# A four-layer graph network on one core: the prologue's order and the written-out order of all jobs of a pair are replaced

## The chip, the cores and the metric

The kernel runs on one core of a Trainium2 chip. The metric is the device time of one execution in microseconds; lower is better. The core has engines that run side by side, each with its own list of instructions that it executes in order: TensorE (PE; PEld is its weight load), VectorE (DVE), ScalarE (ACT), GpSimd (POOL) and SyncE (SP, which issues DMAs). ScalarE issues DMAs too. The engines wait for each other through semaphores only.

## The reference, cut to what matters

Input `x` is 32 graphs of 512 nodes with 64 features, all on one graph matrix `adj` (512 x 512, mostly zeros, symmetric in its zeros but not in its values). Four layers follow one another, each with a layernorm and a relu ahead of it and a residual sum behind it:

```python
# layer 0, three steps, node 0 of v set to the intervention value before
effects = einsum('nm,bmd->bnd', adj, v)
v = relu(concat([v, effects]) @ W1.T + b1) @ W2.T + b2
# layer 1, two steps
z = relu(einsum('mn,bnf->bmf', adj, z) @ weights[i])
# layer 2: eight heads of 64 -> 128, then one of 1024 -> 64
h = x @ W
s = where((h @ h.T) * adj == 0, -1e16, (h @ h.T) * adj)
out = softmax(s) @ h + b            # leaky relu (0.01) behind both
# layer 3, with the diagonal of adj set to 1
e = adj * leaky_relu(e_src[:, None] + e_dst[None, :], 0.2)
out = softmax(e) @ h + bias
```

Everything is float32. Nearly all the work is layer 2: for each graph and head, a 512 x 512 matrix of scores, its softmax, and the weighted sum of values.

## The kernel before, in words

**Tiling.** The 32 graphs are processed as 16 pairs. A pair has a *front* (layers 0 and 1, and the layernorm of layer 2; a generator `front`, L333 to L390, whose 25 steps are called F0 to F24), then eight *units* `Heads` (two graphs times four groups; one unit holds 8 blocks of 64 rows x 512 columns, stored as [128, 8, 512]: two heads of 64 rows each), then the second layer of attention as one unit `Out`, and layer 3 as one unit `Last`. A unit goes through these jobs, each a method of `Unit`, where the letter of the unit's slot is put behind the job's name:

- s0 to s3, `scores` (L427, L430): TensorE makes two row blocks of scores each: four float32 matmuls of 64x64 by 512 a block pair's half (eight in a job) and four bfloat16 matmuls that add a very negative number where the graph is zero, from the tiles I2b (a 64 x 64 identity, twice) and NEGM.
- r0 to r7, `maxima` (L448): VectorE multiplies a block by the graph (A2, in which a zero has been made a one) and takes the row maximum. After every second one POOL negates the two maxima (L455).
- x0 to x3, `exponentials` (L459): ScalarE takes exp with that bias, two blocks a job, and sums rows.
- nA and nB, `normalise` (L469, L471): VectorE's reciprocal of the sums, then four multiplications on POOL.
- t0 to t3, `turn` (L477): VectorE transposes 32 x 32 blocks, two row blocks a job.

Two units together are a `Two`, a sum over nodes numbered by slot (0, 1 for the first graph, 3, 4 for the second): vA to vD, `weigh` (L487), 64 matmuls of 32x64 by 256 each into four PSUM buffers, with the values `vq` as weights; us (L542), four ScalarE copies out of PSUM; w0, y0, w1, y1 (L521, L532), the heads' weight matrices and leaky relu; o and c (L550 to L566), the output projection and its sum in `cat`; then f and h, which make features and node order for `Out`. The values of a graph are 16 small DMAs on SyncE that reorder a tile into quarters of 32 rows (`quarters`, L293, issue L299): ZQ1 does it for the second graph of a pair (the first graph's come with F24), h0 and h1 for `Out`, oN for `Last` (32 there, with four more at L676). `Ends` weighs (L756) an `Out` and a `Last` unit together, as vA2 to vD2, with eu and er behind it; jobs oA to oN are layer 3's layernorm, features and node order. k and Y (L804, L814) multiply the features by the gram matrix G of each head. ZZ1 turns the second graph's features.

**Buffers.** Four PSUM buffers take scores (`ps_s`), four take everything else (`ps_m`, tile name `mm`), in rotation: a job that asks for one waits until the reader of its last occupant is done. Units share three tiles `sm`. Each reordered value tile has one buffer.

**Order.** Nothing is scheduled by a planner at run time. The kernel is cut into ticks, ten to a pair. The table `PLACES` gives for each job a tick, relative to its unit's or pair's own, and a rank. The jobs of a tick are recorded in the order of their ranks, and every engine executes its instructions in the order of the record. The last pair's jobs, and what is left of the pair before it, come in an order of their own, the list `TAIL`, whose tokens have an owner ahead of the colon: a digit for a unit of heads of the last pair, T and U for its sums, p and e for `Out` and `Last` in it, E for `Ends`, and r, q, s for the units that are left behind it.

**Prologue.** The DMAs (L123 to L154): SyncE loads x, the graph A, the net parameters, Wh in two halves, A2, the small vectors, W_out and A3; ScalarE loads W1 and W2 (L132, L133), the biases (L136, L137), the intervention value (L139) and b2 spread over all partitions (L140). Then the first pair's front runs step by step, and `among` names what is put in front of which step: `weights_turned` (transposes of W1 and W2, three copies on ScalarE), `biases`, `weights_joined` (the products W2 W1, and the two bias products), `graph_turned` (sixteen transposes of A into AT, four copies on ScalarE), `masks` (II, I2b, NEGM), `factors` (zeros of A2 into ones), `grams` (G) and `vectors` (layer 3's). The second pair's first six steps run from step 6 on.

Of the kernel before, what the change touches and what calls it, by code (L numbers as in the profile page):

```python
# [9 lines left out]
BF16 = mybir.dt.bfloat16  # L10
AF = mybir.ActivationFunctionType
ALU = mybir.AluOpType
AX = mybir.AxisListType

P = 128
# [6 lines left out]
def gnn_stack_kernel(  # L22
# [107 lines left out]
    for j, r in enumerate(R):  # L130
        for k in range(2):
            nc.scalar.dma_start(out=W1n[r, k, r], in_=W1[:, k * D : (k + 1) * D])  # L132
        nc.scalar.dma_start(out=W2n[r, r], in_=W2)  # L133
    for k, b in enumerate((b1, b2, b_out, bias3)):
        for r in R:
            nc.scalar.dma_start(out=rows[H + k : H + k + 1, r], in_=b.rearrange("(o d) -> o d", o=1))  # L136
    nc.scalar.dma_start(out=rows[0:H, :], in_=bh)  # L137
    for j in range(2):
        nc.scalar.dma_start(out=ivt[:, j, :], in_=iv)  # L139
        nc.scalar.dma_start(out=b2bc[:, 0, j, :], in_=b2.partition_broadcast(P))  # L140
# [27 lines left out]
    I2b = const.tile([P, D], BF16, name="I2b")  # L168
# [13 lines left out]
    def graph_turned():  # L182
        for s in range(NT):
            pt = mm_ps()
            for t in range(NT):
                nc.tensor.transpose(pt[:, blk(t)], A[:, t, blk(s)], ident)
            nc.scalar.copy(AT[:, s, :], pt)
# [7 lines left out]
    def weights_joined():  # L195
        pt = mm_ps()
        for k in range(2):
            nc.tensor.matmul(pt[:, blk(k)], lhsT=W2n, rhs=W1T[:, k, 0, :], start=True, stop=True)
        nc.tensor.matmul(pt[:, 2 * P : 3 * P], lhsT=b2rep, rhs=W1T[:, 1, 0, :], start=True, stop=True)
        nc.tensor.matmul(pt[:, 3 * P : 3 * P + 1], lhsT=W1T[:, 0, 0, :], rhs=b2c, start=True, stop=True)  # L200
        for k in range(2):
            nc.vector.tensor_copy(W1T[:, k, 1, :], pt[:, blk(k)])
        nc.vector.tensor_copy(ubc[:, 0, :], pt[:, 2 * P : 3 * P])
        nc.vector.tensor_tensor(b1s, pt[:, 3 * P : 3 * P + 1], b1c, ALU.add)

    def masks():
# [3 lines left out]
        nc.vector.tensor_copy(I2b, II[:, 0, :])  # L210
# [21 lines left out]
    def grams():  # L232
# [5 lines left out]
        nc.vector.tensor_copy(WT.rearrange("p h d -> p (h d)"), pt)  # L238
# [4 lines left out]
        nc.vector.tensor_copy(G.rearrange("p h d -> p (h d)"), pt)  # L243
# [552 lines left out]
    def keys(ua, ub):  # L796
# [28 lines left out]
        1: [biases, weights_joined, graph_turned],  # L825
        7: [masks],
        8: [lambda: factors(0)],
        9: [lambda: factors(1)],
        10: [lambda: factors(2)],
        11: [lambda: factors(3)],  # L830
        14: [grams],
        15: [vectors],
    }
    for n, _ in enumerate(first):
# [7 lines left out]
        "begina": (0, 20), "s0a": (0, 21), "s1a": (0, 27), "s2a": (0, 97), "s3a": (0, 147), "r0a": (0, 81),  # L842
        "r1a": (0, 139), "r2a": (0, 148), "r3a": (0, 163), "r4a": (0, 214), "r5a": (0, 237),
        "r6a": (0, 242), "r7a": (0, 308), "x0a": (0, 253), "x1a": (0, 293), "x2a": (0, 298), "x3a": (1, 74),
        "t0a": (1, 118), "t1a": (1, 186), "t2a": (1, 285), "t3a": (1, 284), "nAa": (0, 310),
        "nBa": (1, 145), "beginb": (-1, 295), "s0b": (-1, 296), "s1b": (-1, 309), "s2b": (0, 195),
        "s3b": (0, 108), "r0b": (0, 52), "r1b": (0, 54), "r2b": (0, 57), "r3b": (0, 155), "r4b": (0, 234),
        "r5b": (0, 281), "r6b": (0, 226), "r7b": (0, 228), "x0b": (0, 88), "x1b": (0, 255), "x2b": (0, 314),
        "x3b": (0, 252), "t0b": (1, 84), "t1b": (1, 117), "t2b": (1, 102), "t3b": (1, 172), "nAb": (0, 286),
        "nBb": (1, 6), "beginc": (-1, 223), "s0c": (-1, 241), "s1c": (-1, 224), "s2c": (0, 166),  # L850
        "s3c": (0, 170), "r0c": (0, 83), "r1c": (0, 86), "r2c": (-1, 287), "r3c": (0, 37), "r4c": (0, 194),
        "r5c": (0, 248), "r6c": (0, 180), "r7c": (0, 185), "x0c": (0, 178), "x1c": (0, 174),
        "x2c": (0, 302), "x3c": (1, 33), "t0c": (0, 236), "t1c": (0, 299), "t2c": (1, 275), "t3c": (1, 268),
        "nAc": (0, 208), "nBc": (1, 49), "begind": (-1, 273), "s0d": (-1, 274), "s1d": (0, 28),
        "s2d": (0, 136), "s3d": (0, 71), "r0d": (0, 26), "r1d": (0, 46), "r2d": (0, 59), "r3d": (0, 78),
        "r4d": (0, 153), "r5d": (0, 182), "r6d": (0, 140), "r7d": (0, 203), "x0d": (0, 60), "x1d": (0, 163),
        "x2d": (0, 209), "x3d": (0, 238), "t0d": (0, 319), "t1d": (1, 0), "t2d": (1, 29), "t3d": (1, 38),
        "nAd": (0, 262), "nBd": (0, 294), "begine": (0, 41), "s0e": (0, 42), "s1e": (0, 62),
        "s2e": (0, 159), "s3e": (0, 55), "r0e": (0, 44), "r1e": (0, 132), "r2e": (0, 112), "r3e": (0, 152),
        "r4e": (0, 211), "r5e": (0, 216), "r6e": (0, 76), "r7e": (0, 161), "x0e": (0, 204), "x1e": (0, 183),  # L860
        "x2e": (1, 1), "x3e": (0, 258), "t0e": (1, 93), "t1e": (1, 162), "t2e": (1, 212), "t3e": (1, 263),
        "nAe": (0, 246), "nBe": (1, 129), "beginf": (-1, 103), "s0f": (-1, 312), "s1f": (-1, 104),
        "s2f": (0, 87), "s3f": (0, 151), "r0f": (0, 22), "r1f": (0, 77), "r2f": (-1, 239), "r3f": (-1, 261),
        "r4f": (0, 95), "r5f": (0, 179), "r6f": (0, 167), "r7f": (0, 259), "x0f": (0, 250), "x1f": (0, 173),
        "x2f": (0, 272), "x3f": (0, 290), "t0f": (0, 315), "t1f": (1, 43), "t2f": (1, 114), "t3f": (1, 122),
        "nAf": (0, 270), "nBf": (1, 9), "beging": (-1, 256), "s0g": (-1, 257), "s1g": (-1, 277),
        "s2g": (0, 68), "s3g": (0, 2), "r0g": (-1, 297), "r1g": (-1, 301), "r2g": (-1, 307), "r3g": (0, 23),
        "r4g": (0, 169), "r5g": (0, 229), "r6g": (0, 126), "r7g": (0, 142), "x0g": (0, 15), "x1g": (0, 47),
        "x2g": (0, 255), "x3g": (0, 249), "t0g": (0, 300), "t1g": (0, 311), "t2g": (1, 63), "t3g": (1, 64),
        "nAg": (0, 232), "nBg": (0, 260), "beginh": (0, 11), "s0h": (0, 12), "s1h": (0, 39), "s2h": (0, 99),  # L870
        "s3h": (0, 113), "r0h": (0, 75), "r1h": (0, 98), "r2h": (0, 105), "r3h": (0, 115), "r4h": (0, 124),
        "r5h": (0, 164), "r6h": (0, 133), "r7h": (0, 146), "x0h": (0, 100), "x1h": (0, 131),
        "x2h": (0, 215), "x3h": (0, 184), "t0h": (0, 265), "t1h": (1, 65), "t2h": (0, 288), "t3h": (0, 306),
        "nAh": (0, 192), "nBh": (0, 230), "begini": (0, 4), "s0i": (0, 5), "s1i": (0, 8), "s2i": (0, 67),
        "s3i": (0, 106), "r0i": (0, 13), "r1i": (0, 14), "r2i": (0, 16), "r3i": (0, 53), "r4i": (0, 111),
        "r5i": (0, 121), "r6i": (0, 190), "r7i": (0, 191), "x0i": (0, 80), "x1i": (0, 119), "x2i": (0, 235),
        "x3i": (1, 40), "t0i": (1, 89), "t1i": (1, 130), "t2i": (1, 243), "t3i": (1, 271), "nAi": (0, 267),
        "nBi": (1, 90), "beginj": (-1, 221), "s0j": (-1, 222), "s1j": (-1, 289), "s2j": (0, 144),
        "s3j": (0, 120), "r0j": (-1, 279), "r1j": (0, 17), "r2j": (0, 56), "r3j": (0, 61), "r4j": (0, 171),
        "r5j": (0, 254), "r6j": (0, 210), "r7j": (0, 225), "x0j": (0, 109), "x1j": (0, 220),  # L880
        "x2j": (0, 305), "x3j": (0, 280), "t0j": (0, 313), "t1j": (1, 66), "t2j": (1, 72), "t3j": (1, 176),
        "nAj": (0, 264), "nBj": (0, 318), "vA0": (1, 177), "vB0": (1, 198), "us0": (2, 25), "w00": (2, 70),
        "y00": (2, 82), "w10": (2, 127), "y10": (2, 150), "k0": (-1, 321), "Y0": (0, 10), "vA1": (1, 149),
        "vB1": (1, 156), "us1": (1, 282), "w01": (2, 32), "y01": (2, 45), "w11": (2, 134), "y11": (2, 143),
        "k1": (-1, 128), "Y1": (-1, 141), "vA2": (1, 135), "vB2": (1, 168), "vA3": (1, 137),
        "vB3": (1, 219), "us3": (2, 24), "w03": (2, 48), "y03": (2, 94), "w13": (2, 138), "y13": (2, 181),
        "k3": (-1, 187), "Y3": (-1, 189), "vA4": (1, 213), "vB4": (1, 233), "us4": (1, 304), "w04": (2, 34),
        "y04": (2, 85), "w14": (2, 116), "y14": (2, 125), "k4": (-1, 269), "Y4": (-1, 322), "o01": (2, 196),
        "c01": (2, 205), "o03": (2, 188), "c03": (3, 92), "f0": (4, 240), "h0": (5, 51), "o11": (2, 247),
        "c11": (3, 31), "o13": (2, 206), "c13": (3, 3), "f1": (3, 7), "h1": (3, 165), "eu": (2, 79),  # L890
# [159 lines left out]
```

## Time and profile before

| what | value |
|---|---|
| time, median of three runs | 2334.38 us (2334.08 to 2336.33) |
| profiled execution, its own time | 2338.17 us |
| its span, first to last instruction | 2336.3 us |
| mean granted TensorE clock | 0.976 |
| PE busy | 2186.7 us (94%), 32683 matmuls |
| DVE busy | 1857.4 us (80%) |
| ACT busy | 1493.1 us (64%) |
| POOL busy | 1299.6 us (56%) |

The profile is of one execution. A line of it gives a group of instructions or one stretch: start, duration, engine, source line, operation, the tile written and the tiles read (out<-in), their shapes, and how many; in square brackets stands how long the engine was idle before it and what ended that wait. Line numbers are those of the kernel before. A granted clock of 1.00 is TensorE's full speed. A window's row gives the busy time of every engine in that stretch of the span. Busy time of an engine that waits nowhere else is not the whole story: an engine can be idle without any other being the worse for it.

### The profile page before, as it was taken

Reading aid. Unit: us, or ns where it says so; the run is one execution under the profiler, and the core shown is the slowest. Engines: PE = TensorE matmul, PEld = TensorE weight load, DVE = VectorE, ACT = ScalarE, POOL = GpSimd, SP = SyncE. Lnnn points to the kernel's source line nnn. Section 1 sums busy time; section 2 is a strip of 40 time slices with the busy share of each in tenths; the row PEclk is TensorE's granted clock in tenths of the full one; section 3 lists DMA queues with packets and bytes.
Section 4 is the critical chain, followed back from the end, with each engine's and each line's share of the span. In section 5 each row is a group of like instructions: output and inputs, shape, how many; then the busy total and the mean of one; then the engine's idle time right before and its main releaser. Section 6 shows DMA issues by size and latency. Waiting matters only on the chain.

```text
span 2336.3 us, 78517 instructions
## 1 busy us (share of the span) xinstructions
PE 2186.7 (94%) x32683; PEld 1172.3 (50%) x32683; DVE 1857.4 (80%) x4100; ACT 1493.1 (64%) x3752; POOL 1299.6 (56%) x2175
## 2 busy tenths in 40 slices
PE   6889999999999999999999999999999999999863
PEld 3435555555555555555555555555555555555342
DVE  3558788879888888988888898888888898887653
ACT  1346557667676766767676676767666676766544
POOL 2345465656666565565656466565656556655342
PEclk9899999999999999999999999999999999999886
DMA  5001111202121120212112021211202111211112
GB/s 122 11 15 21 25 20 23 42 14 39 21 41 26 24 42 13 41 21 39 25 27 40 13 42 21 37 25 29 39 15 42 20 31 25 31 32 19 22 25 46
DMA packets 279047, 70.20 MB, mean 30 GB/s; under 512 B 275100, under 2 KB 276132, under 8 KB 278692
## 3 DMA queue, kind: packets, MB, share of 16 engines
q1 hardware_dynamic: 277888, 65.02, 16.8%
q8 instruction: 256, 4.19, 0.8%
q14 instruction: 99, 0.81, 0.1%
q10 hardware_dynamic: 804, 0.17, 0.0%
HBM read 10.49 MB, written 4.19 MB: 6 GB/s over the span
## 4 chain that ended last, share of the span: by engine, by line
PE 76%; ACT 9%; DVE 6%; POOL 2%; SPq 2%; issue 1%; DMA 1%; ACTq 0%; DVEq 0%; POOLq 0%
PE s L427 20%; PE mm L487 17%; PE mm L317 9%; ACT sm L459 6%; PE mm L550 5%; PE mm L756 5%; PE mm L521 5%; PE s L430 5%; DVE sm L477 4%; PE mm L329 3%; PE mm L804 3%; SPq L299 2%; PE mm L363 1%; DVE sm L448 1%; PE mm L593 1%
## 5 line engine op out<-in xcount | busy, mean ns | idle before, releaser
L459 ACT ACTIVATE sm<-sm,nmx 128x512 f32<-128x512 f32 x1280 | 911.0, 720 | 238.5 <-POOL nmx L455 238.2
L471 POOL TENSOR_SCALAR sm<-sm,rs 128x512 f32<-128x512 f32 x1280 | 869.8, 699 | 149.1 <-DVE rs L469 109.0
L448 DVE CUSTOM_DVE_ANT_0 sm<-s,A 128x512 f32<-128x512 f32 x1152 | 734.0, 679 | 146.3 <-PE s L430 119.8
L477 DVE STREAM_TRANSPOSE sm<-sm 128x1024 f32<-128x1024 f32 x640 | 769.4, 1224 | 39.5 <-POOL sm L471 38.4
L427 PE MATMUL s<-ZZ,Y 64*64 64x512 f32 x4096 | 572.1, 605 | 24.9 <-ACT Y L814 14.0
L487 PE MATMUL mm<-sm,vq 32*64 32x256 f32 (+1 forms) x17152 | 502.7, 380 | 26.0 <-DVE sm L477 18.3
L455 POOL TENSOR_SCALAR nmx<-mx 128x2 f32<-128x2 f32 x640 | 148.3, 235 | 600.6 <-DVE mx L448 544.7
L487 PEld LDWEIGHTS mm<-sm,vq 32*64 32x64 f32 x17152 | 401.8, 135 | 141.7 <-issue 55.9
L427 PEld LDWEIGHTS s<-ZZ,Y 64*64 64x64 f32 x4096 | 146.9, 132 | 250.2 <-issue 112.9
L430 PE MATMUL s<-NEGM,I2b 64*64 64x512 bf16 x2304 | 257.9, 378 | 0.0
L459 ACT ACTIVATION_READ_ACCUMULATOR sm<-sm,nmx 128x1 f32 x1280 | 251.2, 196 | 0.0
L542 ACT COPY us<-mm 128x256 f32<-128x256 f32 x256 | 76.2, 382 | 156.6 <-PE mm L487 156.4
L317 PE MATMUL mm<-AT,v 128*128 128x512 f32 x384 | 173.6, 595 | 0.0
L532 ACT ACTIVATE y<-mm,cols 128x512 f32<-128x512 f32 x256 | 159.2, 684 | 11.1 <-PE mm L521 11.0
L268 POOL TENSOR_TENSOR xc<-x,nmu 128x512 f32<-128x512 f32 x48 | 54.8, 1141 | 192.1 <-DVE nmu L266 192.1
L430 PEld LDWEIGHTS <-I2b 64*64 64x64 bf16 x2304 | 81.0, 107 | 159.8 <-issue 159.2
L521 PE MATMUL mm<-us,Wh 64*64 64x512 f32 x1024 | 133.9, 592 | 23.1 <-ACT us L542 23.1
L277 POOL TENSOR_TENSOR r<-ve,mhalf 128x8 f32<-128x8 f32 x64 | 110.8, 1731 | 44.9 <-DVE ve L275 41.1
L756 PE MATMUL mm<-sm,vq 32*64 32x256 f32 x3712 | 118.0, 380 | 10.2 <-DVE sm L477 8.8
L550 PE MATMUL mm<-y,Wo_sb 128*64 128x512 f32 x512 | 126.9, 605 | 0.0
L317 PE MATMUL mm<-AT,z 128*128 128x512 f32 x256 | 120.1, 613 | 2.1 <-DVE z L281 1.4
L317 PEld LDWEIGHTS mm<-AT,v 128*128 128x128 f32 x384 | 73.2, 191 | 93.3 <-issue 91.7
(134 smaller groups left out, 2002.0 us busy)
## 6 DMA issues: line engine op xcount, KB each, us to landing
vq<-z SPq DMA_DIRECT2D x512, 32.0 KB, 1.9
vq<-hn SPq DMA_DIRECT2D x512, 32.0 KB, 1.9
vq<-h3n SPq DMA_DIRECT2D x512, 32.0 KB, 1.9
A<-in_adj_dram SPq DMA_DIRECT2D x5, 1024.0 KB
xt<-in_x_dram SPq DMA_DIRECT2D x32, 128.0 KB, 2.3
out_dram<-xo SPq DMA_DIRECT2D x32, 128.0 KB, 2.9
src<-src SPq DMA_DIRECT2D x64, 1.0 KB, 1.9
Wh<-in_L_gnn_Wh_dram SPq DMA_DIRECT2D x2, 256.0 KB
```

Of the source, the lines that this page charges most:

```text
L317: nc.tensor.matmul(pe, lhsT=v[:, m].rearrange("p j d -> p (j d)"), rhs=AT[:, m, :], start=(first and m == 0), stop=(m == NT - 1),)
L427: nc.tensor.matmul(pss[half][R[ab], :], lhsT=lhsT, rhs=rhs, start=True, stop=False)
L430: nc.tensor.matmul(pss[half][R[ab], :], lhsT=I2b[R[half], :], rhs=NEGM[R[half], k, :], start=False, stop=True,)
L448: nc.vector.tensor_tensor_reduce(self.sm[:, s, :], src, graph, 1.0, -FMAX, ALU.mult, ALU.max, self.mx[:, s : s + 1])
L459: nc.scalar.activation(self.sm[:, s, :], self.sm[:, s, :], AF.Exp, bias=self.nmx[:, s : s + 1], accum_out=self.ssum[:, s : s + 1],)
L471: nc.gpsimd.tensor_scalar(self.sm[:, s, :], self.sm[:, s, :], self.rs[:, s : s + 1], 1.0, ALU.mult, ALU.mult)
L477: nc.vector.transpose(out=two, in_=two)
L487: nc.tensor.matmul(self.u[i][R[c], 0 : weights.shape[1] * 32], lhsT=values[32 * i : 32 * i + 32, jb, :], rhs=weights[32 * i : 32 * i + 32, ...
L521: nc.tensor.matmul(py[c][r, :], lhsT=Wh2[R[c], 2 * (self.q - 1 + c) + ab, r], rhs=self.us[R[c], 2 * ab : 2 * ab + 2].rearrange("p i (s e) ...
L532: nc.scalar.activation(y, py[c], AF.Prelu, bias=cols[:, h : h + 1], alpha=0.01)
L550: nc.tensor.matmul(pa[R[ab], :], lhsT=Wo_sb[:, h, :], rhs=self.y[h], start=(k == 0), stop=(k == 1),)
L756: nc.tensor.matmul(self.u[i][r, 0 : N // 2], lhsT=values[i // 2][q, jb, :], rhs=sm[q, :, 32 * jb : 32 * jb + 32], start=(jb == 0), stop=(j ...
```

## The change

Nothing that is computed changes, and no matmul is added or taken away.

- **Loads on ScalarE's queue.** W1's two halves come in one three-dimensional DMA for each half of the partitions (two in all in place of four). The two DMAs of the intervention value move ahead of those of the biases. Behind them ScalarE makes I2b with two copies of 64 rows from the identity; VectorE's cast of I2b in `masks` goes.
- **`graph_turned`** runs ahead of step 1 alone, and its four copies go to ScalarE and VectorE in turns. The products of weights follow at step 2, the biases at step 3, and the bias products, now a function of their own (`biases_joined`), at step 5. `masks` moves from step 7 to 9, the four `factors` from 8 to 11 to 16 to 19, `vectors` from 15 to 17.
- **`grams`** writes its two results with ScalarE, not VectorE.
- **PLACES and TAIL** have new ranks throughout. Most jobs keep their tick. In TensorE's list of a middle pair the differences are few: s0b stands between vB4 and vC4 (behind vD4 before), s2b ahead of w14 and k1, s2f ahead of w01, F18 ahead of s2g, h0 ahead of s0i, oT and oW earlier. On the other engines: ScalarE takes x1g ahead of F18 and x0g behind it (x0g, x1g, F18 before), x3a ahead of us4; VectorE takes the reciprocal of nBe ahead of t0e, c01 behind that of nBd, F13 ahead of r0e; SyncE issues ZQ1 in tick 1 of its pair, not in tick 5.

```diff
-    for j, r in enumerate(R):
-        for k in range(2):
-            nc.scalar.dma_start(out=W1n[r, k, r], in_=W1[:, k * D : (k + 1) * D])
+    for r in R:
+        nc.scalar.dma_start(out=W1n[r, :, r], in_=W1.rearrange("o (k d) -> o k d", k=2))
         nc.scalar.dma_start(out=W2n[r, r], in_=W2)
+    for j in range(2):
+        nc.scalar.dma_start(out=ivt[:, j, :], in_=iv)
+
+    I2b = const.tile([P, D], BF16, name="I2b")
+    for r in R:
+        nc.scalar.copy(I2b[r], ident[r, r])
...
-        nc.scalar.dma_start(out=ivt[:, j, :], in_=iv)
         nc.scalar.dma_start(out=b2bc[:, 0, j, :], in_=b2.partition_broadcast(P))
...
-            nc.scalar.copy(AT[:, s, :], pt)
+            (nc.scalar.copy, nc.vector.tensor_copy)[s % 2](AT[:, s, :], pt)
...
-        nc.tensor.matmul(pt[:, 2 * P : 3 * P], lhsT=b2rep, rhs=W1T[:, 1, 0, :], start=True, stop=True)
-        nc.tensor.matmul(pt[:, 3 * P : 3 * P + 1], lhsT=W1T[:, 0, 0, :], rhs=b2c, start=True, stop=True)
-        for k in range(2):
             nc.vector.tensor_copy(W1T[:, k, 1, :], pt[:, blk(k)])
-        nc.vector.tensor_copy(ubc[:, 0, :], pt[:, 2 * P : 3 * P])
-        nc.vector.tensor_tensor(b1s, pt[:, 3 * P : 3 * P + 1], b1c, ALU.add)
+
+    def biases_joined():
+        pt = mm_ps()
+        nc.tensor.matmul(pt[:, 0:P], lhsT=b2rep, rhs=W1T[:, 1, 0, :], start=True, stop=True)
+        nc.tensor.matmul(pt[:, P : P + 1], lhsT=W1T[:, 0, 0, :], rhs=b2c, start=True, stop=True)
+        nc.vector.tensor_copy(ubc[:, 0, :], pt[:, 0:P])
+        nc.vector.tensor_tensor(b1s, pt[:, P : P + 1], b1c, ALU.add)
...
-        nc.vector.tensor_copy(I2b, II[:, 0, :])
...
-        nc.vector.tensor_copy(WT.rearrange("p h d -> p (h d)"), pt)
+        nc.scalar.copy(WT.rearrange("p h d -> p (h d)"), pt)
...
-        nc.vector.tensor_copy(G.rearrange("p h d -> p (h d)"), pt)
+        nc.scalar.copy(G.rearrange("p h d -> p (h d)"), pt)
...
     among = {
         0: [weights_turned],
-        1: [biases, weights_joined, graph_turned],
-        7: [masks],
-        8: [lambda: factors(0)],
-        9: [lambda: factors(1)],
-        10: [lambda: factors(2)],
-        11: [lambda: factors(3)],
+        1: [graph_turned],
+        2: [weights_joined],
+        3: [biases],
+        5: [biases_joined],
+        9: [masks],
         14: [grams],
-        15: [vectors],
+        16: [lambda: factors(0)],
+        17: [lambda: factors(1), vectors],
+        18: [lambda: factors(2)],
+        19: [lambda: factors(3)],
     }
...
     PLACES = {
...
```

The ranks that the text speaks of, as (tick, rank), before and after: s0b (-1, 296) and (-1, 251); vB4 (1, 233) and (1, 212); vC4 (1, 251) and (1, 269); x0g (0, 15) and (0, 150); x1g (0, 47) and (0, 22); F18 (6, 107) and (6, 103); s2g (0, 68) and (0, 107); s2f (0, 87) and (0, 28); w01 (2, 32) and (2, 29); F13 (4, 73) and (4, 83); r0e (0, 44) and (0, 92); h0 (5, 51) and (4, 310); nBe (1, 129) and (1, 112); t0e (1, 93) and (1, 127); ZQ1 (5, 36) and (1, 91). In TAIL, VectorE's maxima `r:r0f` and `r:r1f` move behind the transposes `p:t2f`, `p:t3f` and `e:t0e`, and unit e's maxima ahead of `p:r0f`:

```diff
-        p:t0f r:x0f p:x2f U:h0 p:nBf r:r4f r:r5f r:x2f r:r7f p:t1f e:t0e p:t3f p:t2f r:x3f r:nBf E:vA2 r:nAf
+        r:r6f r:s0f r:r7f p:nBf r:x2f U:h0 r:r3f r:x3f p:t0f p:t2f p:t3f r:x1f r:r0f r:r1f E:vA2 E:vB2 r:nBf
```

## The prediction

> **What bounds the kernel now.** I read the page's busy table, then the kernel cut into windows, then the waits and the timeline inside those windows where an engine other than TensorE decides.
>
> ```profile
> PE 2186.7 (94%) x32683; PEld 1172.3 (50%) x32683; DVE 1857.4 (80%) x4100; ACT 1493.1 (64%) x3752; POOL 1299.6 (56%) x2175
> ```
>
> TensorE is the bound: 94% of the span. The change removes no matmul, so it can only win TensorE's idle time, or time at a halved clock. The windows say where that is (columns: window, its length, busy time of PE, PEld, DVE, ACT, POOL, granted clock, DMA share, GB/s):
>
> ```profile
> 0.00:74.00 74.00, 42.17 (x185) 25.06 (x185) 23.45 (x46) 10.22 (x18) 20.73 (x29) 0.88 0.44 97
> 74.00:210.00 136.00, 123.83 (x1467) 60.81 (x1470) 91.55 (x207) 71.03 (x179) 67.22 (x125) 0.95 0.11 19
> 618.00:754.00 136.00, 133.49 (x2054) 71.70 (x2046) 115.58 (x255) 93.34 (x236) 81.64 (x136) 1.00 0.18 29
> 2114.00:2250.00 136.00, 112.36 (x1638) 55.25 (x1638) 96.67 (x218) 83.44 (x214) 59.69 (x114) 0.90 0.14 22
> ```
>
> A middle pair of graphs (one period is 135.4 us, thirteen such) keeps TensorE busy for 133.5 of 136 at full clock: about 2.5 us a pair to win, and 115.6 of VectorE close behind. The prologue (42 of 74) and the last pair (112 of 136, clock 0.90) are loose. In the middle pair the waits view gives TensorE's two largest named waits:
>
> ```profile
> PE mm L521 <- ACT us L542: 1.7, 1, 1.7
> PE s L427 <- ACT Y L814: 0.7, 1, 0.7
> ```
>
> In the last pair one DMA wait stands out. SyncE's timeline, then TensorE's:
>
> ```profile
> 2150.47 23.21 SPq L299 DMA_DIRECT2D vq<-h3n  x32
> 2173.78 10.24 SPq L299 DMA_DIRECT2D vq<-z  x16
> ```
> ```profile
> 2179.88 0.65 PE L487 MATMUL mm<-sm,vq 32*64 32x256 f32 x4
> 2180.98 0.61 PE L487 MATMUL mm<-sm,vq 32*64 32x256 f32 x2 [0.46 <-DMA vq<-z]
> 2183.53 6.64 PE L487 MATMUL mm<-sm,vq 32*64 32x256 f32 x122 [1.93 <-DMA vq<-z]
> ```
> ```profile
> 990.60 3.71 PE L487 MATMUL mm<-sm,vq 32*64 32x256 f32 x128
> ```
>
> The sixteen transfers of the second graph's values (job ZQ1) queue on SyncE behind 32 of job oN, are issued only at 2173.78 to 2184.0, and the first half of the weighing vA3/vB3 waits for them. It takes 2179.88 to 2190.09 = 10.2 us. The last line is the same 128 matmuls in a middle pair: 3.6 us to the next instruction. Besides the waits, the clock was 0.50 in 2183.5:2187 and 0.57 in 2187:2190 by the windows.
>
> **The change part by part.**
>
> *ZQ1 from tick 5 of its pair to tick 1.* Sixteen SyncE issues of 0.64 us (10.24/16) now stand ahead of h1 and oN. Their buffer is free after the previous pair's vD4, which ends at 2107.9, so they would be issued by about 2119, and h1, in tick 2, can be issued up to 10 us later; what it loads is weighed in tick 6 (vA2), four ticks of 13.5 us on. oN, in tick 3, finds SyncE free by then. Gain in the last pair: 10.2 - 3.6 = 6.6 us. VectorE does not give it back: after it VectorE waits 6.77 us (2220.68) and 3.11 us (2228.16) for TensorE. Middle pairs: nothing, as 990.60 has no wait on a DMA. Bounds: -6.6, and -2.4 if only the waits (0.46 + 1.93) go and the clock is half anyway. I take -6.4, nearest to the row of the middle pair.
>
> The clock's part leans on the rows: after waits of 2.02 us (ahead of 2176.82) and 1.93 us the clock was 0.50. The Trainium skill ("TensorE: Matmul & The Clock Gate", Part 1) says that the clock halves after an idle window of some 3.4 us, and no single wait here is that long; by that page the slow clock would not be owed to these waits, this step would be worth 2.4 us and the sum -2.3 in place of -6.3. I keep the row.
>
> *The order at the end (TAIL).* Maxima r0f and r1f of the last unit go behind the transposes p:t2f and p:t3f for which E:vA2 waits (8.8 us for VectorE, at 2247.63): two of 0.61 us = -1.2. Against it, six maxima of unit e now go ahead: up to 6 x 0.61 = 3.7 later for the rest, half of it in VectorE's idle 6.77 us. Bounds -3 and +2; I take -1.2. The chain after E:vA2 (88 us to the end) is the same in both.
>
> *Prologue: ScalarE's DMAs and the turned graph.* Two weight DMAs fewer (about 0.3 us each by the issues at L137 to L140); the table load moves off W1T's path:
>
> ```profile
> 12.53 1.28 ACT L179 ACT_TABLE_LOAD   x1 [12.53 <-DMA ivt<-_intervention_value_dram]
> 13.82 0.43 ACT L179 COPY W1T<-mm 128x128 f32<-128x128 f32 x2
> 15.87 3.31 PE L186 MATMUL mm<-ident,A 128*128 128x128 f32 x16
> 19.69 0.59 ACT L311 COPY zT<-mm 128x512 f32<-128x512 f32 x1
> ```
>
> The graph's transposes need only A (9.25) and could go 5 us earlier; the four copies of 0.58 us are shared by two engines. What counts is the zT copy at 19.69, from which the first pair's chain runs. A new wait stands against it: the DMAs for b2bc share, in the program as built, a semaphore lane with Wh's second half and wait on ScalarE for its landing, with W1T, W2T and AT queued behind them. Wh's halves are issued at 12.46 and 13.11 now and landed at 20.4 and 21.5, some 8 us later; issued near 10, as nothing but the DMAs ahead of it on SyncE holds it, the second may land between 13.5 and 18.4. That puts zT 2.8 us earlier to 1.2 later; I take 0.8 earlier. Then biases_joined (matmuls 0.63 + 0.43) stands in the chain: +0.9. Factors move to steps 16 to 19: VectorE's 1.23 + 2.34 at 31.52 and 33.53 no longer hold the second chain: -1.1. Vectors at step 17: one TensorE wait for w3T, +0.65. Grams on ScalarE: -0.1. Removed cast (1.04 at L210): beside other work, 0. Sum -0.45; bounds -2.5 and +1.6; say -0.5. First pairs afterwards: 0 to +1, as their jobs are pulled between the two fronts; +0.3.
>
> *The middle pair's order.* TensorE's list is nearly the same; what differs:
> - s0b (eight matmuls and four masks) goes between vB4 and vC4, where the 256 matmuls were one run of 7.16 us. Split runs with scores between cost 990.60 to 999.11 = 8.51, less 1.23 for the scores = 7.28, and a boundary each: +0.1 to +0.3; I take +0.27, as vC4 starts after a change of tile.
> - ScalarE takes x1g before F18 and x0g after it. x1g waits for POOL's negation at 961.73 (behind nBf, 2.69 us), while x0g ran at 960.84. ScalarE then loses 1.1 us there and has 0.7 of slack before 965.11; x2g ends 0 to 0.5 later, and VectorE's reciprocal for it already waits:
>
> ```profile
> 968.07 0.18 DVE L469 RECIPROCAL rs<-ssum 128x4 f32<-128x4 f32 x1 [1.99 <-ACT sm L459]
> 968.17 4.74 DVE L477 STREAM_TRANSPOSE sm<-sm 128x1024 f32<-128x1024 f32 x4
> ```
>
>  Behind it stand t0g to t3g, r0h to r3h, s3h, F20 and vA3. I take +0.44.
> - Gains: s2f before w01 covers the 1.72 us wait, yet vA2 is held by VectorE's t3f, 0; F18 before s2g frees vA2's PSUM slot (0.6 lost there): half, -0.3; F13 before r0e frees vA1's (0.3): -0.3; h0 before s0i covers Y's 0.7, but vA3 waits for F20 and t1h (7.4 us of VectorE work) anyway: 0.
>
> Sum +0.1 a pair, +1.5 for thirteen. Bounds: -0.6 (both covered waits count too) to +0.71 (no gain comes).
>
> Total: -6.4 - 1.2 - 0.5 + 0.3 + 1.5 = -6.3. The profiled execution took 2338.2 (span 2336.3 + 1.9), 0.16% above the median of 2334.4; the terms are differences, so they go on the median: 2328.1.
>
> **The rivals.**
>
> *A, the loop eats the end.* The gains in the middle pair do not come: +0.71 x 13 = +9.2, and 2334.4 - 7.8 + 9.2 = 2335.8: no change. For it: in ticks 4 to 7 VectorE's chain (t3d, t3f, t3g, r3h) decides and TensorE's small waits fall there, so PSUM slots free earlier may help nobody. Against: 0.6 and 0.3 are waits on slots, not on VectorE.
>
> *B, slower: the reciprocal in front of the transposes.* In tick 5 VectorE now meets nBe's reciprocal ahead of t0e, in the stretch where it is the bound; if it waits for ScalarE there as at 968.07, it loses up to 1.99 us a pair with t0e, t3f and vA2 behind it. It decides from (4.7 + 7.8)/13 = 0.96 us; between the two, 1.5 x 13 = 19.5 gives 2346. Against it: ScalarE is 64% busy, and x2e may be done by then.
>
> *C, the values are hidden anyway.* vA3 needs t1h too, which ends near 2179.8. If the clock stays half for VectorE-bound reasons, only 2.4 is won: 2332.1, no change. For it: the clock is 0.90 over the whole window, so half clock exists without this wait.
>
> **How the numbers follow.** A measurement of this kernel tells 0.2% (4.7 us) from nothing. Forecast 0.45 (faster). A 0.22, of which 0.05 lies over +0.2%. B 0.23. C 0.10. Faster 0.45, same 0.27, slower 0.28. The forecast's own range is 2319 to 2331 (end -9, prologue -2.5 and -0.3 a pair below; +0.3 a pair above). The range reaches down to the end's -9.6 with prologue -2.5 and -0.6 a pair (-20: 2314.5), of which I keep 2315, and up into the lower half of B, 2345; outside lie about 0.06 and 0.12.
>
> **What would show it.** ZQ1: in the last pair, vA3 and vB3 in 3.6 us without a wait on a DMA, and the window at 0.9 clock or more; a half clock there with no wait is C. Loop: the period between two pairs' vA4 against 135.4; at 135.5 my sum is right, at 136.1 A, at 136.4 or more B, with an idle time ahead of L469 in tick 5. x1g: x2g's end against the start of its pair, +0.5. Prologue: zT's copy at about 18.9; W1T's first copy after a wait longer than now is the lane's doing. The forecast is wrong at once if the period moves by more than 0.4 us either way, since thirteen of them outweigh all else.

## The result and the profile after

The changed kernel takes 2343.99 us (median of six, 2340.26 to 2346.80) against 2334.43: ratio 1.0042, 95% interval 1.0031 to 1.0053. It is slower by some 10 us. The forecast was 2328, faster; the time lies inside the range given, 2315 to 2345, but only by what that range allowed for the slower rival B; the forecast's own range was 2319 to 2331.

The same four windows of the profile after (window, length, busy time of PE, PEld, DVE, ACT, POOL, granted clock, DMA share, GB/s):

```profile
0.00:74.00 74.00, 43.42 (x193) 26.18 (x197) 23.09 (x45) 11.17 (x21) 19.72 (x29) 0.86 0.44 98
74.00:210.00 136.00, 125.22 (x1533) 61.63 (x1534) 94.91 (x213) 73.19 (x185) 67.33 (x126) 0.95 0.11 18
618.00:754.00 136.00, 133.91 (x2019) 71.18 (x2003) 115.37 (x255) 93.51 (x235) 80.58 (x135) 1.00 0.18 29
2114.00:2250.00 136.00, 119.59 (x1790) 57.71 (x1790) 101.95 (x227) 85.00 (x217) 64.42 (x120) 0.92 0.13 21
```

The last pair's window is denser (119.6 of 136 busy, not 112.4; it begins 10.6 us earlier within that pair than before), the middle pair's looks the same. The busy share hides the loss; the distance from one pair's vA0 to the next shows it. TensorE's starts of vA0 in the timelines, and the stretches of the last pair, for the kernel before and for two profiled executions of the changed one (us):

| stretch | before | after, first | after, second |
|---|---|---|---|
| first vA0 begins | 107.8 | 105.7 | 108.0 |
| two first periods | 263.3 | 263.4 | 264.8 |
| a middle period, median | 135.29 | 136.31 | 136.30 |
| twelve middle periods | 1624.3 | 1636.1 | 1636.4 |
| last period | 129.5 | 130.4 | 130.7 |
| last pair, vA0 to vA3 | 54.9 | 55.8 | 54.2 |
| vA3 to vA4 | 25.2 | 18.5 | 18.5 |
| vA4 to vA2 of E | 42.5 | 39.7 | 39.6 |
| from there to the last issue on SyncE | 85.9 | 86.2 | 88.0 |

The last pair's vA3 to E's vA2 is 9.5 us shorter, a little more than forecast, and the period is 1.0 us worse, thirteen times. The profiled execution of the kernel before (2338.2) is 2 to 4 us above its medians, so differences of two profiled executions (+2.1 and +6.6) understate the loss; the medians are the measure.

ZQ1 did what was forecast. In the last pair SyncE has no z transfers behind oN's h3n transfers, and the first half of the weighing is one run of 3.71 us without a wait. TensorE's timeline after:

```profile
2191.07 0.38 PE L434 MATMUL s<-NEGM,I2b 64*64 64x512 bf16 x2
2191.38 3.71 PE L491 MATMUL mm<-sm,vq 32*64 32x256 f32 x128
2195.02 1.09 PE L431 MATMUL s<-ZZ,Y 64*64 64x512 f32 x8
```

In the middle pair both of TensorE's named waits are gone, and one of another kind stands there (waits view of after, PE's rows):

```profile
PE s L431 <- DVE mx L452: 1.6, 2, 1.3
PE mm L808 <- ACT ZZ L407: 0.2, 1, 0.2
```

Less is waited for by name (1.8 us against 2.4), and yet the period is longer. The page's chain of work that ended last shows where to look; before, then after:

```profile
PE 76%; ACT 9%; DVE 6%; POOL 2%; SPq 2%; issue 1%; DMA 1%; ACTq 0%; DVEq 0%; POOLq 0%
```
```profile
PE 53%; DVE 17%; ACT 13%; POOL 9%; issue 3%; SPq 3%; DMA 1%; DVEq 0%; ACTq 0%; POOLq 0%
```

The path has moved off TensorE for a fifth of the span: VectorE, ScalarE and POOL have a good part of it, although in the middle pair's window none of them has more to do than before (ScalarE 93.5 us, not 93.3). These shares do not say what it costs: with five orders put back, below, they are PE 65%, DVE 19%, POOL 7% and ACT 4%, and the period is within 0.15 us of the old one.

Laid side by side from vA4 on, two periods part like this: s0b to s1b +0.25; k3 to o03, behind vA1, a further 0.7; then VectorE's t0g is 0.90 later (84.52 us after vA4, not 83.62), F20 0.66 and t1h 0.66 later, and vA3, which waits for t1h, begins at 106.7, not 106.1; o11 adds 0.26. At the next vA4 the sum is 0.92 (1.02 by the medians).

The place behind vA1, ScalarE and TensorE, before and after:

```profile
812.18 1.09 PE L521 MATMUL mm<-us,Wh 64*64 64x512 f32 x8 [1.67 <-ACT us L542]
813.97 2.53 ACT L532 ACTIVATE y<-mm,cols 128x512 f32<-128x512 f32 x4
816.09 1.04 PE L804 MATMUL mm<-ZZ,G 64*64 64x256 f32 x16
817.07 1.94 PE L550 MATMUL mm<-y,Wo_sb 128*64 128x512 f32 x8
```
```profile
811.45 1.35 PE L431 MATMUL s<-HH 64*64 64x512 f32 x6 [1.28 <-DVE mx L452]
815.60 2.42 ACT L536 ACTIVATE y<-mm,cols 128x512 f32<-128x512 f32 x4
816.33 1.67 PE L808 MATMUL mm<-ZZ,G 64*64 64x256 f32 x16
817.93 1.94 PE L554 MATMUL mm<-y,Wo_sb 128*64 128x512 f32 x8
```

ScalarE takes x1f ahead of y01 after the change, so y01 and y11 begin at 815.60, not 813.97. TensorE's k3 (L808) takes 1.67 in place of 1.04 us, as it needs PSUM buffers that y01 empties, and o03 (L554), which multiplies the y, begins 0.86 later (0.99 counted from vA4, which stands at 749.23 before and 749.10 after).

### The profile page after: what moved, and what is told of

Its sections match the earlier page's. It is cut to its first block, busy times and chain, and to the rows that moved or that the text cites. A ratio compares the mean times of both kernels' runs of the same rounds, so it can differ in the third digit from the quotient of the medians.

```text
span 2338.5 us, 78505 instructions
## 1 busy us (share of the span) xinstructions
PE 2204.8 (94%) x32683; PEld 1174.0 (50%) x32683; DVE 1854.2 (79%) x4099; ACT 1503.7 (64%) x3754; POOL 1298.6 (56%) x2175
## 4 chain that ended last, share of the span: by engine, by line
PE 53%; DVE 17%; ACT 13%; POOL 9%; issue 3%; SPq 3%; DMA 1%; DVEq 0%; ACTq 0%; POOLq 0%
PE s L431 14%; PE mm L491 12%; ACT sm L463 9%; PE mm L321 8%; DVE sm L481 7%; DVE sm L452 6%; POOL sm L475 5%; PE mm L554 4%; PE s L434 3%; PE mm L525 3%; PE mm L808 3%; SPq L303 2%; PE mm L333 2%; ACT y L536 1%; PE mm L367 1%
## 5 line engine op out<-in xcount | busy, mean ns | idle before, releaser
L431 PE MATMUL s<-ZZ,Y 64*64 64x512 f32 x4096 | 577.4, 607 | 18.5 <-DVE mx L452 12.9
L491 PE MATMUL mm<-sm,vq 32*64 32x256 f32 (+1 forms) x17152 | 494.9, 378 | 25.4 <-issue 11.0
L491 PEld LDWEIGHTS mm<-sm,vq 32*64 32x64 f32 x17152 | 391.9, 134 | 145.3 <-issue 76.8
L431 PEld LDWEIGHTS s<-ZZ,Y 64*64 64x64 f32 x4096 | 141.9, 132 | 259.5 <-issue 96.8
L434 PE MATMUL s<-NEGM,I2b 64*64 64x512 bf16 x2304 | 268.7, 378 | 0.0
L525 PE MATMUL mm<-us,Wh 64*64 64x512 f32 x1024 | 139.8, 589 | 1.5 <-ACT us L546 1.5
L272 POOL TENSOR_TENSOR xc<-x,nmu 128x512 f32<-128x512 f32 x48 | 55.1, 1148 | 153.6 <-DVE nmu L270 153.6
L554 PE MATMUL mm<-y,Wo_sb 128*64 128x512 f32 x512 | 126.4, 607 | 3.3 <-ACT y L536 3.3
L473 DVE RECIPROCAL rs<-ssum 128x4 f32<-128x4 f32 x320 | 53.9, 168 | 90.0 <-ACT sm L463 89.8
L321 PEld LDWEIGHTS mm<-AT,v 128*128 128x128 f32 x384 | 73.3, 191 | 93.3 <-issue 92.3
```

The lines of the kernel that those rows point to most:

```text
L321: nc.tensor.matmul(pe, lhsT=v[:, m].rearrange("p j d -> p (j d)"), rhs=AT[:, m, :], start=(first and m == 0), stop=(m == NT - 1),)
L431: nc.tensor.matmul(pss[half][R[ab], :], lhsT=lhsT, rhs=rhs, start=True, stop=False)
L434: nc.tensor.matmul(pss[half][R[ab], :], lhsT=I2b[R[half], :], rhs=NEGM[R[half], k, :], start=False, stop=True,)
L491: nc.tensor.matmul(self.u[i][R[c], 0 : weights.shape[1] * 32], lhsT=values[32 * i : 32 * i + 32, jb, :], rhs=weights[32 * i : 32 * i + 32, ...
L525: nc.tensor.matmul(py[c][r, :], lhsT=Wh2[R[c], 2 * (self.q - 1 + c) + ab, r], rhs=self.us[R[c], 2 * ab : 2 * ab + 2].rearrange("p i (s e) ...
L554: nc.tensor.matmul(pa[R[ab], :], lhsT=Wo_sb[:, h, :], rhs=self.y[h], start=(k == 0), stop=(k == 1),)
```

## The experiments

**The changed kernel again, and two orders put back.**

```diff
-"x1f": (0, 31)     "s2f": (0, 28)
+"x1f": (0, 225.5)                       # e1 and e3
+                   "s2f": (0, 29.5)     # e2 and e3
```

> The changed kernel once more, for a second profile of it: its first profiled execution (2340.3 us) is the fastest of its six times (2340.3 to 2346.8). Theory P (the loss sits in the period of a middle pair, 136.3 against 135.3 us): the period is 136.3 again or a little more, and a slower time comes from longer periods (5 us over 13 pairs = 0.4 each). Theory V (the loss of the slower times sits at the ends, in prologue and last pair, where the granted clock is below 0.95): all periods 136.3 as before and the ends longer by up to 6 us.

> The changed kernel, with ScalarE's x1f put back behind y11 (rank 225.5 for 31). Theory X (x1f of 1.5 us ahead of y01 keeps two PSUM buffers that k3 waits for: k3 begins 0.24 and o03 0.86 us later than in the kernel before): the period falls from 136.3 by 0.8 to 0.9, to 135.4 or 135.5, and the time by some 11 us to 2333. Theory S (s2f ahead of w01 is the loss, since it waits 1.28 us for VectorE with w01 behind it): the period stays at 136.2 or more, and the time within 2 us of the changed kernel's.

> The changed kernel, with TensorE's s2f put back behind w01 (rank 29.5 for 28). Theory X: the period moves by at most 0.3, as k3 still waits for y01; time within 4 us of the changed kernel's. Theory S: the period falls by 0.8 or more, to 135.5 or less, and the time by 10 us or more.

> The changed kernel with both put back. Theory X: as with x1f alone, 135.4, or up to 0.3 less; time 2330 to 2333. Theory S: as with s2f alone. If neither is the loss, the period stays at 136.3.

| kernel | period | time | ratio to before |
|---|---|---|---|
| after, again | 136.30 | 2346.49 | 1.0043 (1.0028 to 1.0058) |
| x1f back | 136.05 | 2342.11 | 1.0024 (1.0014 to 1.0034) |
| s2f back | 136.96 | 2359.38 | 1.0096 (1.0081 to 1.0111) |
| both back | 136.92 | 2355.76 | 1.0088 (1.0072 to 1.0103) |

The second profile has the same period; what differs between executions lies at the ends (the first vA0 at 105.7 or 108.0, the last stretch 86.2 or 88.0). So P holds for the loss, and V, by these two profiles, for the scatter. Theory S falls with the wrong sign: s2f ahead of w01 is a gain of 0.65 us a period in this order (0.87 with x1f back as well), though its row shows a wait of 1.28 us that was not there before. Theory X has the right sign and a third of the size: 0.25, not 0.8 to 0.9; its bound on s2f, 0.3, does not hold either. With x1f back, o03 begins at 67.9 us after vA4, as before the change (67.8); 0.9 us are won there, and by vA3 0.6 of them are lost again. That a gain on TensorE vanishes before vA3 is the observation on which the next theory rests: that from there to vA3 VectorE sets the time.

**One order each, and five together.**

```diff
-"s0b": (-1, 251)  "x0j": (0, 138) "x1j": (0, 109)  "t0e": (1, 127)    "x0g": (0, 150)
+"s0b": (-1, 277.5)                                                    # e4, e9
+                  "x0j": (0, 109) "x1j": (0, 138)                     # e7, e9
+                                                   "t0e": (1, 111.5)  # e8, e9
+                                                                      "x0g": (0, 21.5)  # e9
+"x1f": (0, 225.5)                                                     # e9
```

> The changed kernel, with s0b put back behind vD4. Theory D (a period is one stretch that TensorE bounds, from vA3 to s0f, and one that VectorE bounds, from there to vA3; what is lost in either is paid in full, and TensorE's waits inside VectorE's stretch cost nothing): s0b's 0.25 us stands in TensorE's stretch, so the period falls from 136.30 to 136.05. Theory E (the period is TensorE's list with its waits added up): the same 0.25 less, so that this run alone does not tell them apart; it sets the price of the split.

> The changed kernel, with ScalarE's x0j and x1j exchanged, so that x0j stands ahead of y13 as before. x1j waits 0.91 us for POOL's negation there and y13, then o11 on TensorE, are 0.26 late. Theory D: that lies in TensorE's stretch, period 136.04. If the wait is taken over by another (k0, F6): 136.3.

> The changed kernel, with VectorE's t0e put back ahead of nBe's reciprocal, which waits 0.36 us for ScalarE at 65.2 of the period. Theory D: it lies in VectorE's stretch, and 0.14 to 0.36 of it come off the period: 135.9 to 136.2, though no wait of TensorE names it. Theory E: no change, 136.30, as no wait of TensorE goes.

> The changed kernel with five orders of the middle pair put back: s0b behind vD4, x1f behind y11, x0j ahead of x1j, t0e ahead of nBe, x0g ahead of x1g. The rest of PLACES, TAIL, ZQ1 and the prologue stay. Theory D: 136.30 less 0.25 (s0b), 0.25 (x1f, as measured), 0.26 (x0j), 0.14 to 0.36 (t0e) and 0 to 0.17 (x0g) gives 135.0 to 135.4, as before the change; then the changed ends are left, -6 to -8 us: ratio to the kernel before 0.9966 to 0.9980. Theory E: TensorE keeps the gains at vA1 and vA2 (0.55 and 0.24), which makes 134.6 to 134.9 and a ratio of 0.993 to 0.995.

The periods are 136.01 (s0b back), 136.11 (x0j first), 136.35 (t0e first) and 135.44 (all five). Each of the three single ones has one execution; the five measured 2332.81, ratio 0.9986 (0.9977 to 0.9996).

So s0b between vB4 and vC4 costs 0.30, x1j ahead of x0j 0.20, x1f ahead of y01 0.25: 0.75 of the 1.0. The last two are in the timeline of after: x1f above, and here x1j, ScalarE's wait for POOL, with y13 behind it, for which TensorE's o11 waits:

```profile
869.19 0.72 ACT L463 ACTIVATE sm<-sm,nmx 128x512 f32<-128x512 f32 x1 [0.91 <-POOL nmx L459]
870.62 1.24 ACT L536 ACTIVATE y<-mm,cols 128x512 f32<-128x512 f32 x2
871.67 1.51 PE L554 MATMUL mm<-y,Wo_sb 128*64 128x512 f32 x6
```

t0e, ahead of the reciprocal or behind it, is worth nothing in the changed kernel: with t0e first VectorE's wait of 0.36 us ahead of nBe goes, one of 0.30 comes behind r5f, its wait for TensorE's s0g ahead of r0g grows from 0.19 to 0.26, and r0g begins at 72.03 us after vA4, not 72.01. TensorE's late s0g (x1f, y, o03) set that time, not the reciprocal. The other 0.1 is left to x0g and the interplay of the five, by difference. In the kernel with five back t0g stands 83.66 us behind vA4, as before the change (83.62), and its period is 0.15 longer than before's. Theory E, by which TensorE would keep what it gained at vA1 and vA2, asked for 134.6 to 134.9 and falls, also when it is granted that of vA2's 0.55 only 0.34 was left (134.8 to 135.1). Theory D's 135.0 to 135.4 is just missed; its account of t0e was wrong.

Where the gains went shows in the starts from vA4 on (medians of twelve periods; five back, then before): vA1 52.33 and 52.37, vA2 79.11 and 79.01, vA3 106.02 and 105.97. In the changed kernel they are 52.68, 80.19 and 106.73. So in the kernel with five back vA1 and vA2 became shorter, and vA2 and vA3 did not begin earlier. Busy shares alone would not have told this; the stretch from vA1 to vA3, before and after:

```profile
936.50:991.00 54.50, 51.99 (x818) 27.53 (x818) 49.63 (x111) 39.77 (x100) 32.81 (x55) 1.00 0.24 42
```
```profile
937.40:992.00 54.60, 52.71 (x806) 27.86 (x798) 49.15 (x111) 39.90 (x99) 32.76 (x55) 1.00 0.19 34
```

TensorE is the busier one in it, and VectorE itself waits in it, 2.0 us for ScalarE ahead of t0g. That VectorE's chain sets the time there is argued from the starts; t0e put back, which takes a wait out of that chain, gained nothing.

**The ends alone, on the kernel before.**

```diff
-"ZQ1": (5, 36)
+"ZQ1": (1, 36)      # e6, e11, e12; new TAIL in e11 and e12, new prologue in e10 and e12
```

> The kernel before, with ZQ1 alone moved from tick 5 to tick 1. Prediction's step: the last pair's vA3 and vB3 take 3.6 in place of 10.2 us, nothing else moves, the time is 6.4 us less: ratio 0.9972. Rival C (only the waits go, at half a clock): 2.4 less, 0.9990.

> The kernel before with the new prologue alone (loads, order, copies, grams), PLACES and TAIL as before. In the profiles the first vA0 began at 105.7, 106.4 and 108.0 us in kernels with the new prologue and at 107.8 before. Theory N: the prologue is worth 0 to -2 us in every execution, ratio 0.9991 to 1.0000. Theory V: the executions without a profile, which are slower than the profiled one with the new prologue (2346.5 against 2344.8; 2332.8 against 2327.1) and not with the old one (2334.4 against 2338.2), lose 3 to 6 us there: ratio 1.001 to 1.003.

> The kernel before with ZQ1 in tick 1 and the new TAIL; prologue and PLACES as before. By the profile of the changed kernel its last pair and what follows it are 8.4 us shorter than before's. Theory N and V alike: 7 to 9 us less, ratio 0.9962 to 0.9970. If the new TAIL needs the new PLACES to be good: as with ZQ1 alone, 0.9972, or worse.

> The same with the new prologue. Theory N: a further 0 to 2 us less, ratio 0.9955 to 0.9970. Theory V: 3 to 6 us more than with the old prologue, ratio 0.9975 to 0.9995.

| kernel | time | ratio to before |
|---|---|---|
| ZQ1 alone | 2331.45 | 0.9980 (0.9969 to 0.9990) |
| prologue alone | 2335.73 | 1.0003 (0.9993 to 1.0012) |
| ZQ1 and TAIL | 2330.50 | 0.9978 (0.9968 to 0.9987) |
| ZQ1, TAIL and prologue | 2332.34 | 0.9986 (0.9977 to 0.9995) |

ZQ1 with the new TAIL has the lowest time of all; it beats the kernel before and the changed one, but is not told apart from ZQ1 alone. 7 to 9 us were expected of it, and it won 5. ZQ1 alone is worth 4 to 5 us, between the step (6.4) and rival C (2.4), and its interval reaches both: vA3 to vA4 went from 25.2 to 18.7 as forecast, but vA0 to vA3 grew from 54.9 to 57.9 or 58.0 in all three kernels that have ZQ1 in tick 1 of the old PLACES. There TensorE's clock was lower behind a wait of the same 1.80 us for VectorE. Windows around vA1, before and with ZQ1 alone:

```profile
2148.00:2153.00 5.00, 3.20 (x22) 0.59 (x12) 5.00 (x8) 2.99 (x8) 1.64 (x4) 0.90 0.18 14
2153.00:2157.00 4.00, 4.00 (x102) 2.92 (x108) 3.00 (x10) 2.04 (x6) 1.22 (x4) 0.70 0.33 53
```
```profile
2145.00:2150.00 5.00, 3.20 (x18) 0.69 (x12) 5.00 (x8) 3.04 (x8) 1.51 (x4) 0.84 0.19 15
2150.00:2154.00 4.00, 4.00 (x75) 2.44 (x80) 2.86 (x10) 2.12 (x6) 1.35 (x4) 0.50 0.35 58
```

That costs 1.5 of the 3 us. The other 1.5 come behind the next wait, one of 2.02 us ahead of vA3 in both kernels: the clock behind it was 1.00 in 2175:2179 before, and 0.69 in 2176:2181 with ZQ1 alone.

The new prologue is worth nothing that can be measured. Alone it lies between the ranges of theories N and V; on top of ZQ1 and TAIL the time is 1.8 us higher, within the intervals, so neither theory is shown. In the profiles its first vA0 begins at 105.7 to 108.1 us, the old one's at 105.1 to 108.2.

**PLACES alone, ZQ1 elsewhere, and one more order.**

```diff
+PLACES of the changed kernel, "ZQ1": (5, 91); the rest as before     # e13
+the kernel before, new TAIL, "ZQ1": (3, 0)                           # e14
+the five of e9, and "oW": (8, 269) for (7, 166)                      # e15
```

> The kernel before with the new PLACES alone, but ZQ1 left in tick 5; prologue and TAIL as before. By the profiles the order of the middle pair is worth +1.0 us in each of thirteen periods and +0.9 in the first two pairs: 13 to 15 us, ratio 1.0056 to 1.0064, period 136.3. If the order loses more than the profiles show (the changed kernel's median is +9.6 to +10.4, its parts in the profiles add up to +5 to +7): ratio 1.007 or more. If the new PLACES is only bad together with the new prologue or TAIL: below 1.005.

> The kernel before with the new TAIL and with ZQ1 in tick 3, behind h1 and ahead of oN on SyncE. With ZQ1 in tick 1 the last pair's vA3 and vB3 were 6.5 us shorter but vA0 to vA3 took 58 in place of 54.9 us, at a granted clock of 0.50 against 0.70 around vA1. If those 3 us are owed to ZQ1's early place: 54.9 again, 3 us better than with tick 1, ratio 0.9962 to 0.9970. If they are a matter of where the clock's drop falls: 54 to 58, ratio 0.9970 to 0.9985.

> The changed kernel with the five orders put back and oW too (directly ahead of oN). With five back the period is 135.44, 0.15 above before's. oW ahead of f1 puts 0.86 us of TensorE work ahead of w00, so ScalarE's y00, x1d and then VectorE's t0d come 0.3 to 0.6 later, at the head of VectorE's stretch. Theory D: the period falls to 135.3 or less; the ratio falls by 0.0005 to 0.001 against the five's 0.9986. If t0d is not on the chain: 135.44.

| kernel | period | time | ratio to before |
|---|---|---|---|
| PLACES alone | 136.41 | 2345.68 | 1.0045 (1.0030 to 1.0060) |
| ZQ1 in tick 3, TAIL | 137.32 | 2357.12 | 1.0092 (1.0077 to 1.0107) |
| six orders back | 136.99 | 2354.10 | 1.0078 (1.0061 to 1.0095) |

PLACES alone loses 10 us, where 13 to 15 were expected; nothing beyond its period (twelve of them 12.9 longer) is needed for it. In its profile vA3 to vA4 is 22.3, not 25.2, which takes 3 off.

ZQ1 in tick 3 was expected to be the best and costs 21.6 us. Its 16 transfers stand ahead of oN's four on SyncE, and the Prelu of the next `Last` unit waits for these four. In that kernel, SyncE, then ScalarE, then TensorE's vA1:

```profile
930.18 11.01 SPq L299 DMA_DIRECT2D vq<-z  x16
941.29 2.62 SPq L676 DMA_DIRECT2D src<-src  x4
```
```profile
944.61 1.84 ACT L699 ACTIVATE sm<-pd,src 128x512 f32<-128x512 f32 x3 [2.39 <-DMA src<-src]
```
```profile
946.68 0.69 PE L487 MATMUL mm<-sm,vq 32*64 32x256 f32 x15 [1.44 <-DVE x L370]
```

vA1 waits for F13 on VectorE, which in the old PLACES stands behind r0e, which waits for that Prelu. In that kernel the queue of transfers is thus on the path of every pair: 11.01 us of issue time ahead of four small transfers cost 2 us a period.

oW back ahead of oN costs 1.55 us a period, where a gain of 0.15 was expected. TensorE then stands at the first matmul of F12:

```profile
936.09 1.06 PE L666 MATMUL mm<-w3a,zT 128*128 128x130 f32 x8
938.53 1.12 PE L367 MATMUL mm<-hT,W1T 128*128 128x512 f32 x2 [1.39 <-ACT h3T L657]
```

F12 needs the PSUM buffer that oW filled, and ScalarE copies it out only behind its exponentials. oW's earlier place is a gain in the new order, and the last 0.15 us of the period stay open; 0.1 of it lies between vA3 and vA4 (29.43 us with five back, 29.32 before).

## Why the prediction was wrong

*ZQ1, -6.4.* Right at its place: -6.7 by the last pair's vA3 to vA4, no wait on a DMA, a run of 3.71 us. Of the two bounds the upper was the true one, so the slow clock there did go with the waits. As for the Trainium skill's rule ("TensorE: Matmul & The Clock Gate", Part 1), that an idle window of about 3.4 us is needed for the slow clock: the rows here show 0.50 behind waits of 1.80 and 1.93 us. One reading of the prediction was wrong: behind the wait of 2.02 us ahead of 2176.82 the clock was still 1.00, until 2182; the 0.50 came behind the waits for the DMAs. In the kernel with ZQ1 alone the clock took 3 us back elsewhere, part of it behind that same wait; in the changed kernel it did not (55.8 and 54.2). Rival C is refuted in the changed kernel; by the time of ZQ1 alone it is not excluded.

*TAIL, -1.2.* vA4 to E's vA2 fell by 2.8 in the changed kernel, and the stretch behind it, which the prediction took as unchanged, rose by 0.3 and 2.1; by the medians (2331.45 to 2330.50) TAIL is worth 1.0, near the 1.2 forecast, but the intervals do not tell it from nothing.

*Prologue, -0.5.* The copy of zT came at 17.98, not 19.69, earlier than the forecast 18.9. The wait on ScalarE that was named came too: the DMAs for b2bc were issued at 14.14, when Wh's second half had landed (14.12), and W1T's copy behind them began at 15.04, not 13.82. But the matmuls behind zT took almost twice as long and gave the gain back; the granted clock was 0.50 in 16:22, and 1.00 there before. TensorE and ScalarE after:

```profile
15.04 0.43 ACT L182 COPY W1T<-mm 128x128 f32<-128x128 f32 x2 [8.58 <-DMA early<-in_L_gnn_bh_dram]
17.98 0.59 ACT L315 COPY zT<-mm 128x512 f32<-128x512 f32 x1 [1.36 <-PE mm L313]
18.62 2.08 PE L333 MATMUL mm<-W1T,zT 128*128 128x128 f32 x8 [0.47 <-ACT zT L315]
21.20 1.85 PE L367 MATMUL mm<-zT,W1T 128*128 128x512 f32 x2
```

The same matmuls took 1.16 and 1.02 us before. In the second profile of the changed kernel they took 2.08 and 2.05 while its clock reads 1.00 there, so the clock as the cause rests on the first and on the new prologue alone (0.50 in 18:24). Nothing is left: 1.0003.

*The middle pair, +0.1 a period.* This is the step that failed; it measured +1.0, which is thirteen times 0.9 beyond the sum, more than all the rest. Its terms:

- s0b between vB4 and vC4, forecast +0.27: measured 0.30. Right.
- F18 ahead of s2g, which frees vA2's PSUM slot, -0.3, and F13 ahead of r0e, which frees vA1's, -0.3. The stalls did go (vA1 takes 1.78 us, not 2.02; vA2 1.78, not 2.33), but the period did not get them. With five orders back vA1 is 0.24 and vA2 0.34 shorter than before the change, and vA2, vA3 and the next vA4 begin no earlier; the period is 135.44. The prediction took a shorter stall of TensorE for a shorter period, in a stretch where TensorE only came earlier to its next wait. Neither order was put back alone. Without the two gains the prediction's own sum is -7.8 + 9.2 = +1.4. Rival A said so, at +0.71 a period and 2335.8, and is nearest by its cause; rival B's 2346 is nearer by the number.
- x1g ahead of F18, forecast +0.44: VectorE's wait at the reciprocal of nBg grew from 1.99 to 2.16. Small, and not tested alone.
- "s2f before w01 ... 0": in the new order it is worth 0.65 a period, as putting it back shows.
- Not in the sum at all: x1f ahead of y01 (0.25) and x1j ahead of x0j (0.20). Both are ScalarE's order, of which only x1g was weighed; together they are 5.9 us in thirteen periods. o03 reads y 2.3 us after y01 begins, and k3 wants its buffers sooner still.

Rival B named the right verdict with the wrong place: nBe's reciprocal does wait ahead of t0e, 0.36 us, far from the 0.96 from which it decides, and t0e put back gave 136.35, no gain.

What stays open: 0.15 us of the period, why the clock drops more behind the same two waits in the last pair with ZQ1 moved alone, and what in the lists makes single periods 1 to 2 us longer in some executions (one of 138.15 in the kernel with s0b back).

## What to carry to other kernels

Where one engine is 98% busy in a window and another 85%, ask stretch by stretch which of them the next stretch waits for, before adding up waits: a wait of the busiest engine inside another's stretch can be worth nothing, and a job of an idle-looking engine that stands ahead of what the busiest reads soon after can be paid (x1f: 0.25 of the 0.9 us by which o03 was late; x1j: 0.20 of 0.26). When a table of orders is replaced as a whole, compare every engine's list, not TensorE's alone, and take it in parts: here ZQ1 and TAIL were worth -5 us (-3 with the new prologue), PLACES alone +10, and the kernel with the lowest time has only ZQ1 and TAIL.

## What was not expected of the hardware

The granted clock behind the same wait (1.80 us) was 0.70 in one kernel and 0.50 in another, for 4 us, and behind the next (2.02 us) 1.00 and 0.69, with the same work on TensorE behind it; the time that a gain at the ends brings depends on where such a drop falls. Two of the maxima of a `Last` unit, with both operands in SBUF, take 1.52 us, the others 0.68. In after these are 26 of 128. Each of the two runs beside an operation of POOL on a tile of the same size and ends about 0.55 us after it: the first (803.56 to 805.08) after the xc of L272, which ends at 804.53, the second (805.01 to 806.52) after the squaring, which ends at 805.98. The third has no such operation beside it (VectorE and POOL after):

```profile
803.56 1.52 DVE L452 CUSTOM_DVE_ANT_0 sm<-sm,A 128x512 f32<-128x512 f32 x1
804.61 1.37 POOL L274 TENSOR_TENSOR sq<-xc 128x512 f32<-128x512 f32 x1
806.46 0.68 DVE L452 CUSTOM_DVE_ANT_0 sm<-sm,A 128x512 f32<-128x512 f32 x1
```
